# Constant products ahead of TensorE's waits in a Fourier-attention layer

## The chip, the cores and the metric

The kernel runs on one core of one Trainium2 chip. The metric is device time in microseconds (us) of one execution. A core has a matrix engine (TensorE, "PE" in the profile, with its weight loads as "PEld"), three elementwise engines (VectorE "DVE", ScalarE "ACT", GpSimd "POOL"), a queue engine (SyncE "SP") and 16 DMA engines. TensorE reads SBUF and writes PSUM. TensorE's clock is granted by a throttle: the profile shows the share granted, 1.00 or less.

## The reference

The input is `x` of shape (4, 32, 128, 128). Layer 0 is a Fourier neural operator with attention over the 32 images (128 x 128) of each of the four batch elements; layer 1 is an additive attention and a mixture of experts over 4096 tokens per batch element. Only layer 0 matters here:

```python
xn = _inorm(xa, norm1_w, norm1_b)
k = _fno_layer(xn, Kcw, Ksw, Hs, Ws); q = _fno_layer(xn, Qcw, Qsw, Hs, Ws)
v = _fno_layer(xn, Vcw, Vsw, H, W)
scores = jnp.einsum('bntk,bnsk->bnts', qf, kf) / (np.float32(np.sqrt(Hs * Ws)) * temperature)
p_attn = jax.nn.softmax(scores, axis=-1)
av = jnp.einsum('bnts,bnsk->bntk', p_attn, vf)
p = _fno_layer(av, Pcw, Psw, H, W)
a = _inorm(p + xa, attn_w, attn_b)
an = _inorm(a, norm2_w, norm2_b)
m = _fno_layer(an, m0cw, m0sw, H, W, inner_norm=True, act=True)
m = _fno_layer(m, m1cw, m1sw, H, W, inner_norm=True, act=False)
out = _inorm(m, mon_w, mon_b) + a
```

Each `_fno_layer` is a 2-D Fourier transform cut to a block of modes, a product with complex weights, and the transform back, plus a scaled copy of its input. The kernel does the transforms as products with matrices of cosines and sines, and works out the scores and the means and variances from the modes. All of it is float32.

## The kernel before, in words

`layer0` runs a loop over the four batch elements `b` (the loop begins at L687). For one `b` it goes through these stages, all on the 32 images of that element:

- attention-weighted values (`po`, L778): five blocks of modes, in each of which VectorE and GpSimd multiply modes with weights (`u`) and TensorE sums over the images with the probabilities `pr`; `cm` (L703) and the skips (`pxt` L723, `sk` L742) go with it;
- back to space (`py` L798, then `inverse`, L273 and L278), and the statistics of the sum `q`;
- the first inner layer: `spectra` (`pz` L248, `px` L871), then `weighed` (L894), in which VectorE reduces the weighed squares to `v_s` and TensorE sums over the partitions (`ms`, in `sums`, L314); then `back` (L288): products `y` (L297) into two wide PSUM tiles, a copy `v` to SBUF by ScalarE or VectorE, the product `four` (L308), and `gelu` by VectorE and ScalarE;
- the same for the second inner layer, with the next element's statistics (`image_sums`, whose matrix sums are `mg`, `bg` and `my`) and modes (`spectra_of_images`: `pz`, `px` L263 and L264) and its attention (`attention_weights`) between its parts; then `back` again with `last`, which adds to the output image.

`attention_weights` makes the scores. For each of 17 mode columns VectorE makes a tile `pa`, and VectorE (every third column) or GpSimd (the others) a tile `pb` (L522, L524), of 32 x 32 products of modes; TensorE sums both over the modes into `sp` (L528), four products of 32 rows each. `pa` and `pb` share six SBUF buffers, one of which holds `sod` through the stage. Then come `sc`, the softmax, and a way through DRAM (`prd`) that gives `pr`.

The statements are Python, but their order on the engines is not the text's: a scheduler places the instructions of layer 0 on each engine's queue, from its own estimates of when each is ready. Each queue then runs strictly in that order. A PSUM tile that is asked for under a tag (`a`, `b` and `wide`, two buffers each) waits until an older tile of that tag has been read. The orders on the queues that are told below are those of the built programs. Layer 1 has an order written out by hand, and is not touched.

In the first pass, before the loop, the weights for the values are prepared on VectorE (L469 to L479) beside the first element's statistics and modes, and the first attention.

Of the kernel before, what the change touches and what calls it, by code (L numbers as in the profile page):

```python
# [7 lines left out]
F32 = mybir.dt.float32  # L8
# [5 lines left out]
P = 128  # L14
# [94 lines left out]
def layer0(  # L109
    tc, x, kq_modes, kq_mirror, vcw, pcw, mcols, mcol0, mrows, heads, heads_row, small_row, by_p, inv_cols, dram, x1, first  # L110
):
    nc = tc.nc
# [174 lines left out]

    def back(spec, a, take):  # L288


        wide = [ps.tile([P, 2, 512], F32, name="y1", tag="wide") for _ in range(2)]
        for slot in range(4):
            c = slice(slot * P, slot * P + P)
            for k, trig in enumerate((cos_back, sin_back)):
                for g in range(4):
                    r = slice(32 * g, 32 * g + 32)
                    nc.tensor.matmul(  # L297
                        wide[g // 2][:, g % 2, c],
                        spec[r, 4 * a + slot, 64 - 64 * k : 192 - 64 * k],
                        trig[r],  # L300
                        start=k == 0,
                        stop=k == 1,
                    )
        for g in range(4):
            v = grp.tile([P, 4, C], F32, name="v1", tag="v", bufs=3)
            evacuate(v.rearrange("p k c -> p (k c)"), wide[g // 2][:, g % 2])
            four = ps.tile([P, 4, C], F32, name="four", tag="b")
            nc.tensor.matmul(four, inv, v, start=True, stop=True)  # L308
            take([image(a, g, k) for k in range(4)], four)

    def sums(name, matrix, src):

        m = ps.tile(list(src.shape), F32, name=name, tag="wide")
        nc.tensor.matmul(m, matrix, src, start=True, stop=True)  # L314
        return m

# [3 lines left out]
    def image_sums(b, xt):  # L320


        rows8 = ps.tile([64, 4, C], F32, name="rows8", tag="wide")
        for g in GROUPS:
            xx2 = grp.tile([P, GI, C], F32, name="xx2", tag="pr", bufs=6)
            nc.scalar.activation(xx2, xt[:, g : g + GI], AF.Square)
            for h in range(2):
                m = g // 4 + h
                for k, src in enumerate((xt[:, 4 * m : 4 * m + 4], xx2[:, 4 * h : 4 * h + 4])):
                    nc.tensor.matmul(  # L330
                        rows8[32 * k : 32 * k + 32],
                        one_of_8[:, 7 - m : 39 - m],
                        src,
                        start=m == 0,
                        stop=m == 7,
                    )
        ev = grp.tile([64, 4, C], F32, name="ev", tag="v", bufs=3)
        nc.scalar.copy(ev, rows8)
        s12 = ps.tile([P, 2, 512], F32, name="s12", tag="wide")[:, :, :T]
        for j in range(4):  # L340
            for k in range(2):
                r = slice(32 * k, 32 * k + 8)
                nc.tensor.matmul(s12[:, k, j::4], ev[r, j], ident[r, r], start=True, stop=True)
        sv = small.tile([P, 2, T], F32, name="sv", tag="pk_sq")
        nc.vector.tensor_copy(sv, s12)

        tot = one("tot", 2)
        nc.vector.tensor_reduce(tot, sv, AX.X, ALU.add)
        mg = sums("mg", group, tot)
        gm = one("gm")  # L350
        nc.vector.tensor_copy(gm, mg[:, 0:1])
        gv = one("gv")
        nc.vector.tensor_mul(gv, gm, gm)
        nc.vector.tensor_tensor(gv, mg[:, 1:2], gv, ALU.subtract)
        gr, _ = inv_std("gn_r", gv, 1)
        gs = one("gs")
        nc.vector.tensor_mul(gs, gm, gr)

        both = small.tile([P, 2, 32], F32, name="both", tag="both")
        nc.vector.tensor_scalar(both[:, 0], of_group, gr, None, ALU.mult)  # L360
        nc.vector.tensor_scalar(both[:, 1], of_group, gs, -1.0, ALU.mult, ALU.mult)
        by_group = small.tile([P, 2, 32], F32, name="by_group", tag="by_group")
        nc.vector.tensor_copy(by_group, sums("bg", ones, both))
        n = 1 + 2 * KY
        colg = small.tile([P, 2, n], F32, name="colg", tag="colg")
        nc.vector.tensor_scalar(colg[:, 0], cols1[:, :n], gr, None, ALU.mult)
        nc.vector.tensor_scalar(colg[:, 1], cols2[:, :n], gr, None, ALU.mult)
        m128 = one("m128")
        nc.vector.tensor_scalar(m128, gm, 128.0, None, ALU.mult)

        gs128 = one("gs128")
        nc.vector.tensor_scalar(gs128, gs, 128.0, None, ALU.mult)
        gg = one("gg")
        nc.vector.tensor_mul(gg, gs, gs128)
        gr2 = one("gr2")
        nc.vector.tensor_mul(gr2, gr, gr)
        grs = one("grs")
        nc.vector.tensor_scalar(grs, gs, gr, -2.0, ALU.mult, ALU.mult)
        y12 = small.tile([P, 2, T], F32, name="y12", tag="pk")
        nc.vector.tensor_scalar(y12[:, 0], sv[:, 0], gr, gs128, ALU.mult, ALU.subtract)  # L380
        nc.vector.tensor_scalar(y12[:, 1], sv[:, 1], gr2, gg, ALU.mult, ALU.add)
        nc.vector.scalar_tensor_tensor(
            y12[:, 1], sv[:, 0], grs, y12[:, 1], ALU.mult, ALU.add
        )
        nc.vector.tensor_scalar(y12, y12, 1.0 / NPIX, None, ALU.mult)
        my = sums("my", ones, y12)
        ym, yv = per_image("ym"), per_image("yv")
        nc.vector.tensor_copy(ym, my[:, 0])
        nc.vector.tensor_mul(yv, ym, ym)
        nc.vector.tensor_tensor(yv, my[:, 1], yv, ALU.subtract)  # L390
        yr, _ = inv_std("n1_r", yv)
        ysc = scalars(ALU.mult, "n1_s", yr, par[:, N1W : N1W + 1])
        return by_group, colg, m128, ysc
# [93 lines left out]
    def attention_weights(b, front):  # L487
# [23 lines left out]
        )  # L511

        sp = ps.tile([P, T, 16], F32, name="sp", tag="b")
        for yy in range(KA):
            xs_p = xp[:, yy].unsqueeze(2).to_broadcast(tt)
            xs_s = xm[:, yy].unsqueeze(2).to_broadcast(tt)
            pa = grp.tile(tt, F32, name="pa", tag="pr", bufs=6)
            pb = grp.tile(tt, F32, name="pb", tag="pr", bufs=6)
            for k, t in enumerate((pa, pb)):
                other = xm[:, k * KA + yy].unsqueeze(1).to_broadcast(tt)  # L520
                if k == 0 or yy % 3 == 2:
                    nc.vector.tensor_tensor(t, xs_p, other, ALU.mult)  # L522
                else:
                    nc.gpsimd.tensor_tensor(t, xs_s, other, ALU.mult)  # L524
            for j, (wt, pp, h) in enumerate(
                (w, p, h) for w, p in ((w_re, pa), (w_im, pb)) for h in range(2)
            ):
                nc.tensor.matmul(  # L528
                    sp[32 * j : 32 * j + 32],
                    wt[:, yy],  # L530
                    pp[:, :, 16 * h : 16 * h + 16],
                    start=yy == 0,
                    stop=yy == KA - 1,
                )
# [152 lines left out]
    for b in range(B):  # L687
# [12 lines left out]
        for h in range(2):  # L700
            r = slice(32 * h, 32 * h + 32)
            cm = ps.tile([P, T, 16], F32, name="cm", tag="a")
            nc.tensor.matmul(cm, pv[r].to_broadcast([NH, P]), ph[r], start=True, stop=True)  # L703
            cd = grp.tile([P, T, 16], F32, name="cd", tag="v", bufs=3)
            nc.vector.tensor_tensor(cd, cm, sel.unsqueeze(2).to_broadcast([P, T, 16]), ALU.mult)
            nc.vector.tensor_reduce(
                cp[:, 16 * h : 16 * h + 16], cd.rearrange("p s t -> p t s"), AX.X, ALU.add
            )
# [42 lines left out]
        for x0 in range(0, KX, NK):  # L751
            nk = min(NK, KX - x0)
            m = nk * KY
            po = ps.tile([P, NK * KY], F32, name="po", tag="a")[:, :m]
            for i in range(4):
                xb = late.tile([P, 2, NK * KY], F32, name="xb", tag="xb")[:, :, :m]
                for r in range(2):
# [133 lines left out]
                nc.scalar.activation(spec[:, s4, :64], spec[:, s4, P:], AF.Copy, scale=-1.0)  # L891
            return spec, sq

        def weighed(name, sq, squares, weights):  # L894

            t = sq[:, 1]
            by_row, by_column = weights
# [15 lines left out]
                ALU.mult,  # L913
            )
            nc.vector.scalar_tensor_tensor(by_t, squares, by_column, by_t, ALU.mult, ALU.add)
            m = sums("ms", ones, by_t)
            out = per_image(name)
            nc.vector.tensor_copy(out, m)
            return out


        spec, sq = spectra(0, q)
        v0 = weighed("v0", sq, squares, layers[0][2])
        nc.vector.tensor_mul(v0, v0, r2)
        nc.vector.tensor_mul(v0, v0, r2)
        r0, ve = inv_std("r0", v0)
# [40 lines left out]
        spec, sq = spectra(1, gl)  # L967
        if b + 1 < B:
            front = spectra_of_images(b + 1, loaded, normed)
        v1 = weighed("v1", sq, squares, layers[1][2])  # L970
        vc = weighed("vc", sq, squares, layers[1][3])
        r1, _ = inv_std("r1", v1)
        s1 = par[:, S1 : S1 + 1]
        nc.vector.tensor_mul(vc, vc, r1)
# [671 lines left out]
```

## Time and profile before

| | |
|---|---|
| median of 3 runs | 3178.72 us (3177.18 to 3182.71) |
| profiled execution, its own time | 3191.62 us |
| span of the profiled execution | 3189.9 us |
| mean granted TensorE clock, whole span | 0.953 |
| layer 0, 0 to 1105 us: TensorE busy, clock | 934.2 us, 0.87 |
| layer 1, 1105 to 3189.9 us: TensorE busy, clock | 1994.5 us, 0.99 |

The profile is of one execution. Its parts are the busy time of each engine by slice of the span, the waits of an engine with what ended them, the timeline of an engine's instructions (start, duration, engine, line, operation, out<-in, shapes, count, and in brackets the idle time before it and what ended that), and the busy time by stretch. In the waits the columns are the total, the number and the longest. A float32 product has two records in the trace, so a count of x16 is eight products. Ends of products are modelled; starts are not.

### The profile page before, as it was taken

To read this page: it belongs to the slowest core of one execution; us is meant where nothing else is said; L and a number is where in the kernel's file an instruction comes from. 1 tells how busy PE (TensorE), PEld (TensorE's weight loads), DVE (VectorE), ACT (ScalarE), POOL (GpSimd) and SP (SyncE) were. 2 spreads that over 40 slices of the span, in tenths; PEclk is the share of its full clock that TensorE was granted. 3 is DMA by queue.
4 is the path that set the end of the run, shared out by engine and by line. 5 is a ranking of instruction groups with operands and counts; after the bars stand their busy time and mean duration, and the time that the engine had idled before them with its cause. 6 is when DMAs were issued, how large, how long until landed. Compare 5 with 4: busy or idle time off the path is not lost.

```text
span 3189.9 us, 53099 instructions
## 1 busy us (share of the span) xinstructions
PE 2928.7 (92%) x19634; PEld 1438.2 (45%) x19634; DVE 2290.9 (72%) x5035; ACT 2311.7 (72%) x3138; POOL 2102.7 (66%) x1831
## 2 busy tenths in 40 slices
PE   7888798798888789999999999999999999999997
PEld 5366365345546444444344443444444444444443
DVE  5876666667677566777666868866778777687887
ACT  2344243253343589998999999998999999999992
POOL 1621540460451289878788797889878889888773
PEclk6998998899898799999999999999999999999998
DMA  6301310130140211010111010011010011101000
GB/s 140 111 18 30 95 50 3 49 123 1 30 130 2 57 31 31 8 31 7 31 37 24 14 24 14 8 39 31 23 29 9 14 37 24 37 1 31 14 14 14
DMA packets 152308, 112.77 MB, mean 35 GB/s; under 512 B 36878, under 2 KB 140657, under 8 KB 151441
## 3 DMA queue, kind: packets, MB, share of 16 engines
q1 hardware_dynamic: 136209, 103.61, 12.2%
q10 hardware_dynamic: 15840, 5.77, 0.8%
q8 instruction: 155, 2.54, 0.3%
q14 instruction: 104, 0.85, 0.1%
HBM read 68.37 MB, written 20.00 MB: 28 GB/s over the span
## 4 chain that ended last, share of the span: by engine, by line
PE 61%; POOL 12%; ACT 9%; DVE 9%; issue 7%; DMA 1%; ACTq 0%; POOLq 0%; DVEq 0%; SPq 0%
PE d L1446 19%; PE po L1465 11%; PE px L1352 6%; ACT r L1496 4%; PE po L778 4%; PE n L1446 3%; POOL e L1505 3%; POOL e L1504 3%; PE pz L248 2%; PE four L308 2%; ACT e L1512 2%; PE px L871 1%; PE sk L742 1%; POOL kx L1111 1%; DVE r L1501 1%
## 5 line engine op out<-in xcount | busy, mean ns | idle before, releaser
L1501 DVE TENSOR_TENSOR r<-n,r 128x1024 f32<-128x1024 f32 (+1 forms) x1056 | 961.6, 952 | 479.0 <-PE n L1446 389.4
L1504 POOL TENSOR_TENSOR e<-r 128x512 f32<-128x512 f32 x528 | 673.2, 1275 | 268.1 <-DVE r L1501 267.6
L1496 ACT ACTIVATE r<-d 128x1024 f32<-128x1024 f32 (+1 forms) x1056 | 792.9, 802 | 67.4 <-PE n L1446 56.4
L1508 ACT ACTIVATE r<-r 128x1536 f32<-128x1536 f32 x528 | 783.6, 1484 | 16.8
L1505 POOL TENSOR_TENSOR e<-e,r 128x512 f32<-128x512 f32 x528 | 671.3, 1271 | 41.4
L1446 PE MATMUL d<-qe,ke 32*128 32x512 f32 (+3 forms) x2304 | 605.8, 602 | 39.6 <-ACT r L1496 36.5
L1465 PE MATMUL po<-e,kx 128*128 128x512 f32 (+3 forms) x1152 | 594.5, 605 | 15.6 <-POOL e L1517 15.6
L1446 PE MATMUL n<-qe,ke 32*128 32x512 f32 (+3 forms) x2304 | 606.2, 601 | 0.0
L1446 PE MATMUL n<-qf,kf 32*128 32x512 f32 (+3 forms) x2304 | 552.6, 554 | 0.0
L1446 PE MATMUL d<-qf,kf 32*128 32x512 f32 (+3 forms) x2304 | 550.2, 553 | 0.0
L1356 DVE SCALAR_TENSOR_TENSOR xc<-px,wgt,xc 128x128 f32<-128x128 f32 x1024 | 358.1, 350 | 42.2 <-PE px L1352 9.7
L1512 ACT ACTIVATE e<-e 128x512 f32<-128x512 f32 x528 | 325.8, 617 | 66.2 <-POOL e L1505 65.6
L1465 PEld LDWEIGHTS po<-e,kx 128*128 128x128 f32 x1152 | 175.5, 188 | 392.8 <-issue 306.9
L1446 PEld LDWEIGHTS d<-qe,ke 32*128 32x128 f32 x2304 | 176.5, 183 | 359.3 <-ACT r L1496 339.5
L773 POOL TENSOR_TENSOR u<-xb,gb 128x858 f32<-128x858 f32 (+1 forms) x120 | 233.1, 1968 | 139.5 <-PE po L778 128.0
L1446 PEld LDWEIGHTS d<-qf,kf 32*128 32x128 f32 x2304 | 220.2, 186 | 176.1 <-issue 163.8
L1352 PE MATMUL px<-we,x2t 128*128 128x512 f32 x512 | 264.0, 601 | 6.8 <-DVE xc L1356 6.0
L775 DVE TENSOR_TENSOR u<-xw,gb 128x858 f32<-128x858 f32 (+1 forms) x200 | 206.6, 1082 | 59.2 <-PE po L778 46.6
L885 POOL TENSOR_TENSOR spec<-part,part 128x512 f32<-128x512 f32 x16 | 24.8, 1550 | 333.4 <-ACT z L188 75.2
L1446 PEld LDWEIGHTS n<-qf,kf 32*128 32x128 f32 x2304 | 228.3, 185 | 19.2 <-issue 11.4
L778 PE MATMUL po<-u,pr 128*32 128x429 f32 (+1 forms) x1280 | 191.1, 548 | 26.8 <-DVE u L775 11.7
L524 POOL TENSOR_TENSOR pb<-xm 128x1024 f32<-128x1024 f32 x48 | 90.7, 1913 | 159.1 <-ACT xm L457 152.8
(388 smaller groups left out, 3953.9 us busy)
## 6 DMA issues: line engine op xcount, KB each, us to landing
xb<-xd SPq DMA_DIRECT2D x128, 214.5 KB
xc<-x SPq DMA_DIRECT2D x29, 512.0 KB
x<-x SPq DMA_DIRECT2D x16, 512.0 KB
qf<-qe SPq DMA_DIRECT2D x64, 128.0 KB
out<-xc SPq DMA_DIRECT2D x15, 512.0 KB
xb<-xd SPq DMA_DIRECT2D x32, 198.0 KB
gb<-gd SPq DMA_DIRECT2D x4, 1056.0 KB
x<-in_x SPq DMA_DIRECT2D x8, 512.0 KB
```

What stands on the lines that cost most here:

```text
L773: nc.gpsimd.tensor_tensor(u, xb, gk, ALU.mult)
L778: nc.tensor.matmul(po[32 * j : 32 * j + 32], pr[:, i, k], u[:, r], start=i == 0 and k == 0, stop=i == 3 and k == 1,)
L1352: nc.tensor.matmul(px, x2t[:, k * P : (k + 1) * P], we[:, e0 : e0 + 4], start=True, stop=True)
L1356: nc.vector.scalar_tensor_tensor(xc[:, k], px[:, e], wgt[:, k, e0 + e : e0 + e + 1], xc[:, k], ALU.mult, ALU.add)
L1446: nc.tensor.matmul(o, k, q, start=turn == 0 or g > 0, stop=turn == 1 or g > 0)
L1465: nc.tensor.matmul(sums[c, h][:, q0 : q0 + c1 - c0], kx[:, jb], e[:, c0:c1], start=jb == 0, stop=is_last and q0 > 2 * P, skip_group_check= ...
L1496: nc.scalar.activation(r[:, g], d, AF.Ln, scale=1.0 / DSCALE)
L1501: nc.vector.tensor_tensor(r[:, g], part, r[:, g], ALU.mult)
L1504: nc.gpsimd.tensor_tensor(e, r[:, 1], r[:, 2], ALU.add)
L1505: nc.gpsimd.tensor_tensor(e, e, r[:, 0], ALU.add)
L1508: nc.scalar.activation(r, r, AF.Exp, scale=-1.0)
L1512: nc.scalar.activation(e, e, AF.Exp)
```

## The change

A function `hold(tile, n)` issues `n` products of two constant matrices (`rows` and `inv`, 128x128) into a PSUM tile that a later product overwrites. It is called in six places: ahead of the first `four` of each `back` (3), ahead of `bg` for the first element (18, into a tile of their own), for each of the 17 columns of `attention_weights` (4, into a tile `beside` of tag `b` that nobody reads), ahead of the two `cm` of the first element (26 and 8), ahead of the first block of `po` (14), and ahead of `ms` in the first inner layer and, for the last element, the second (24, the tile then being 128 columns wide instead of 32). In all 548 products are added:

| tile | products |
|---|---|
| `beside` | 272 |
| `ms` | 120 |
| `po` | 56 |
| `four` | 48 |
| `cm` | 34 |
| `early` | 18 |

No other instruction is added or removed; the scheduler's order changes in places on every engine.

```diff
             four = ps.tile([P, 4, C], F32, name="four", tag="b")
+            if g == 0:
+                hold(four[:, 0], 3)
             nc.tensor.matmul(four, inv, v, start=True, stop=True)
...
-    def sums(name, matrix, src):
+    def hold(tile, n):
+
+        for _ in range(n):
+            nc.tensor.matmul(tile, rows, inv[:, : tile.shape[-1]], start=True, stop=True)
+
+    def sums(name, matrix, src, idle=0):
 
-        m = ps.tile(list(src.shape), F32, name=name, tag="wide")
+        m = ps.tile([P, P] if idle else list(src.shape), F32, name=name, tag="wide")
+        if idle:
+            hold(m, idle)
+            m = m[:, : src.shape[-1]]
         nc.tensor.matmul(m, matrix, src, start=True, stop=True)
         return m
...
+        if b == 0:
+            hold(ps.tile([P, P], F32, name="early", tag="wide"), 18)
         nc.vector.tensor_copy(by_group, sums("bg", ones, both))
...
         sp = ps.tile([P, T, 16], F32, name="sp", tag="b")
+        beside = ps.tile([P, P], F32, name="beside", tag="b")
         for yy in range(KA):
+            hold(beside, 4)
...
             cm = ps.tile([P, T, 16], F32, name="cm", tag="a")
+            if b == 0:
+                hold(cm.rearrange("p s t -> p (s t)")[:, :P], 26 - 18 * h)
...
             po = ps.tile([P, NK * KY], F32, name="po", tag="a")[:, :m]
+            if x0 == 0:
+                hold(po[:, :P], 14)
...
-        def weighed(name, sq, squares, weights):
+        def weighed(name, sq, squares, weights, idle):
...
-            m = sums("ms", ones, by_t)
+            m = sums("ms", ones, by_t, idle)
...
-        v0 = weighed("v0", sq, squares, layers[0][2])
+        v0 = weighed("v0", sq, squares, layers[0][2], 24)
...
-        v1 = weighed("v1", sq, squares, layers[1][2])
-        vc = weighed("vc", sq, squares, layers[1][3])
+        v1 = weighed("v1", sq, squares, layers[1][2], 24 * (b + 1 == B))
+        vc = weighed("vc", sq, squares, layers[1][3], 0)
```

## The prediction

> **What bounds the kernel now.** I read the page's slices of the span first, then the waits of TensorE inside the first 1110 us, then TensorE's timeline and the busy time by stretch. The change touches layer 0 alone, which ends near 1105 us.
>
> ```profile
> PE   7888798798888789999999999999999999999997
> PEclk6998998899898799999999999999999999999998
> ```
> From about slice 15 on TensorE is full and its clock granted; before that the clock is short in most slices. The waits of TensorE in that part:
>
> ```profile
> PE ms L314 <- DVE v_s L915: 31.3, 5, 6.3
> PE sp L528 <- POOL pb L524: 23.6, 16, 2.4
> PE po L778 <- DVE u L775: 11.7, 4, 5.2
> ...
> PE cm L703 <- DVE ph L564: 9.5, 4, 7.7
> ...
> PE bg L314 <- DVE both L361: 4.5, 1, 4.5
> ```
> These are the "known waits": five of about 6 us for `ms`, four of 3 to 5 us for `po`, one of 7.7 for `cm`, one of 4.5 for `bg`, sixteen short ones for `pb`. What follows them is in the busy time by stretch (PE, PEld, DVE, ACT, POOL, then clock, DMA share, GB/s):
>
> ```profile
> 32.00:66.00 34.00, 32.41 (x148) 31.64 (x148) 15.72 (x59) 3.43 (x8) 0.00 (x0) 0.50 0.52 114
> 66.00:97.00 31.00, 28.11 (x172) 7.28 (x171) 29.25 (x37) 3.97 (x6) 23.37 (x13) 0.81 0.47 107
> 229.00:256.00 27.00, 24.73 (x179) 11.37 (x180) 22.10 (x95) 16.93 (x39) 0.00 (x0) 0.83 0.00 1
> 306.00:344.00 38.00, 28.32 (x178) 7.81 (x178) 28.41 (x32) 15.70 (x37) 33.53 (x17) 0.77 0.08 21
> 486.00:521.00 35.00, 32.43 (x176) 18.40 (x178) 23.21 (x98) 18.34 (x40) 0.00 (x0) 0.64 0.00 0
> ```
> At half clock TensorE looks busy because its products take twice as long. Only in 32:66 is TensorE itself the bound. In 229:256 and 486:521 (the gelu stage of the first two images) VectorE and ScalarE work beside it; in 66:97 (attention of the first batch element) VectorE is full, and in 306:344 (that of the second) GpSimd is.
>
> Durations come from TensorE's timeline:
>
> ```profile
> 190.64 1.96 PE L273 MATMUL pv<-cst,yf 128*66 128x128 f32 x16 [1.00 <-ACT yf L188]
> 192.44 2.02 PE L278 MATMUL four<-icol,v 66*128 66x128 f32 x16
> ...
> 260.90 0.62 PE L871 MATMUL px<-z,cst 128*32 128x256 f32 x2
> 261.45 0.49 PE L248 MATMUL pz<-cst,g 128*128 128x128 f32 x2
> 261.87 1.06 PE L871 MATMUL px<-z,cst 128*32 128x256 f32 x20
> ...
> 328.05 0.62 PE L528 MATMUL sp<-pb,w_im 128*32 128x512 f32 x2 [0.80 <-POOL pb L524]
> 328.06 0.62 PE L528 MATMUL sp<-pa,w_re 128*32 128x512 f32 x2
> 328.50 0.60 PE L528 MATMUL sp<-pb,w_im 128*32 128x512 f32 x2
> 328.52 0.60 PE L528 MATMUL sp<-pa,w_re 128*32 128x512 f32 x2
> 328.93 0.60 PE L528 MATMUL sp<-pb,w_im 128*32 128x512 f32 x2
> ```
> A product has two records. Eight 128x128 products in a row take 192.44 - 190.64 = 1.80 us, 0.225 each; a lone `pz` between two narrow `px` takes 261.87 - 261.45 = 0.42, so 0.2 more. The lone `px` of 256 columns takes 0.55; `sp` runs its four 32-row products of 512 columns side by side in 0.88 (328.05 to 328.93), so 256 columns should be 0.43: another 0.12. A lone full-width product inside narrow ones thus costs 0.225 + 0.32.
>
> **The Trainium skill.** "TensorE: Matmul & The Clock Gate", Part 1, "What's actually happening": the clock is halved by default and is released by about 3.4 us of activity, lost after an idle window. The trace agrees on 1.00 and 0.50, but in 32:66 the clock stays at 0.50 though products of 67 columns follow one another: not every busy stretch releases it. The same page, "LDWEIGHTS (loading the stationary operand)": the load's time is set by the columns of the weights; the trace agrees, since `px` of 67 columns is 0.22 at full clock, like the 0.225 above. Part 3, "The mechanism": products start and end in program order; so an added product that runs late delays the one that it stands ahead of. The trace shows no product out of the program's order. "Why this matters for your kernels" asks for no idle gap over about 3 us; here a gap of 2.2 us (317.9 to 320.1) already cost the clock.
>
> **The change, part by part.** 548 full-width products are added: 126 us of TensorE at 0.23, twice that at half clock.
>
> *Waits for `ms`* (24 each, 5 waits). 24 x 0.23 = 5.5 us inside 6.0 to 6.3: free, and the clock should be whole when `y` and `four` follow. Worth: VectorE's waits for `four` while the clock is low. In 229:256 these are 0.16 + 0.88 + 0.21 = 1.2 us; in 486:521 they sum to 11.3 against 4.4 in 229:256, so 7 there; about 2 in each of the later two. VectorE's `v` and `x` instructions stand in fixed order before the first `g` (it would start at 235.6 instead of 235.7), so the rest of the 4 us that TensorE saves is idle time. TensorE then idles 2 us before the third `four`, and may lose the clock again, as at 494 us: I take 8 of the 12. The fifth wait (1064 to 1070) is followed by gaps of 2.5 and 4.1 us for `v`, which throw the clock away again: -2 (0 to -8, from 12 us of lost cycles in 1070:1105).
>
> *`po`* (14, 4 times): 3.2 us in waits of 3 to 5.2; lost cycles after them are 1.3, 2.9 and 1.7 us, half on the path: -3. *`four`* (3, 16 times): 0.42 + 2 x 0.225 = 0.87 against a wait of 0.3 to 0.6 after the copy of `v`; where VectorE is the bound nothing is lost, in the second use of `back` about 0.3 each: +2.
>
> *`beside`* (4 for each of 17 columns, 4 times). In the changed order on TensorE, 9 stand before `so`, 12 between `so` and the first `sp`, and 47 among the `sp` in 20 groups; in four columns a group also stands between `pa` and `pb`, which then no longer run side by side. `beside` takes the PSUM buffer of the last `px`, so it starts when VectorE has copied that, at 306.5, when `so` starts now; and the clock is at half there. 9 x 0.45 = 4.05, `so` 1.5, 12 holds 2.9 (clock back by then): first `sp` near 315 instead of 311.9. From there 13 x 0.86 + 4 x 1.72 = 18.1 for `sp`, 47 x 0.225 = 10.6, 20 x 0.32 = 6.4: 35.1 us, ends at 350.1; now 343.4. GpSimd's own work (12 `pb` of 1.9, 4 adds of 2.35: 32.3 from 309.0) no longer covers it: TensorE becomes the bound. Softmax, `y`, `four` and `po` queue behind `sp` on TensorE, VectorE's `mx` behind `pa`: all move by 7. Three times: +21. What is unmeasured is the cost of a lone hold among `sp`: without any switching cost 28.7 us, end 344 to 346 with GpSimd's waits: +1 to +2.5 each; with the groups at half clock much more.
>
> *First batch element.* The 18 `early` fill 19.2 to 23.3; `bg` comes at 23.4 instead of 30.6, since VectorE's chain to `both` is now ahead of the value weights. But `my` now stands before `px`, and waits for `y` behind six 32x1088 instructions of 0.7 to 1.27 us: near 33. TensorE is idle from 24.6, the clock is lost as before, `px` starts 2 us later, and 8 `pz` (0.45 each) come later: `so` 4.4 us later if the clock stays low; 7 us earlier if the run of 11 `pz` (5 us) brings it back. Then `sp`: 35.1 us in place of 25 (72.2 to 97.0). Less 2.3 us (constants on VectorE kept `mx` from 101.1 to 103.5, now done meanwhile) and 2 us of full clock for `cm` and `po` (27 holds, 6.2 us in a wait of 7.7): +13 in the one case, -1 in the other; I take +6.5.
>
> Sum: 6.5 + 21 + 2 - 8 - 3 - 2 = +16.5 us. Queues of DMA issues change little: the loads of layer 1's `spare` move two places ahead of `xb`, `prd` behind two more copies of `xw` on ScalarE (1 us, inside the above).
>
> **Time.** The profiled execution took 3191.6 us (span 3189.9), the median of the three runs is 3178.7. 3191.6 + 16.5 = 3208; on the median 3195.
>
> **Rivals.** (1) *Faster: a lone hold costs only its 0.225 and the clock stays whole.* Then `sp` is covered by GpSimd again: 3 x 2.5 + 1, gelu stage -12, `po` -4, the last element -8, `four` 0: about -16, median 3163. It decides where the switch costs under about 0.1 us. For it: the sums above lean on five lone `pz`; against: each of those shows 0.42. 0.25.
> (2) *No change to speak of:* the first element gains its clock (-1), switching costs half (3 x 4), gains as taken: -1 + 12 + 2 - 13 = 0, 3179. 0.15.
> (3) *The change does not do what it says:* the holds do not keep the clock, gelu gains nothing: 13 + 27 + 2 = +42, 3221; if they stay at half clock inside `sp`, an attention stage takes 13 x 1.7 + 4 x 3.4 + 47 x 0.45 + 6 = 63 us, over +100 in all. The lone half-clock stretch 32:66 speaks for it, against it that the 3.3 us of `pz` from 822 us brought the clock back. 0.15. The forecast itself: 0.45.
>
> By itself the forecast's case runs from 3185 (first element -1, TensorE's stream two us shorter) to 3206 (first element +13). The range 3160 to 3226 leaves out the tails of (1) and (3). A difference of 0.2% (6.4 us) is about what a measurement of this kernel can tell from none. Faster 0.25, same 0.15, slower 0.60.
>
> **What would show it.** Right: no idle of TensorE before `ms`, clock 1.00 in the gelu stages; `sp` in each attention stage 35 us long with waits of VectorE and GpSimd for `sp` grown from some 6 and 0.7 us; a lone hold of 0.4 us. Wrong: `sp` still ending with GpSimd's last `pb`, or the clock back in 32:66.

## The result and the profile after

| | before | after |
|---|---|---|
| median | 3179.22 us (3177.18 to 3182.71) | 3205.37 us (3204.40 to 3207.38) |
| ratio, 95% interval | | 1.0082 (1.0064 to 1.0099) |
| profiled execution, its own time | 3191.62 us | 3205.44 us |
| end of layer 0 in it | 1104.4 us | 1116.9 us |
| rest of the span | 2085.5 us | 2086.8 us |

The changed kernel is 26 us slower. Of the 13.8 us between the two profiled executions 12.5 lie in layer 0; layer 1 is nearly as long in both. The profiled execution of before lies 12 us above its median, that of after on its median, so the two traces show only half of the difference; how far executions of one kernel differ is taken up below, at the kernel before once more. One execution of the kernel before among those of the experiments, 3229.20 us at a clock of 0.913 where its others have 0.950 to 0.965, is in a slower state and is left out of every comparison.

The slices of the span of after: first TensorE's busy share, then its granted clock.

```profile
PE   7999999999999889999999999998999999999997
PEclk9999999999999899999999999999999999999998
```

In the first 15 slices the clock's digits 6 and 8 of before have become 9, and its 7 an 8: the products do what they are there for, TensorE is fuller and its clock is granted. The kernel is slower all the same. The waits of TensorE in 0 to 1140 us (total, number, longest):

```profile
PE four L309 <- DVE v L190: 13.3, 8, 2.7
...
PE my L323 <- DVE y L396: 7.7, 1, 7.7
...
PE po L795 <- DVE u L792: 4.1, 5, 1.1
...
PE ms L323 <- DVE v_s L932: 3.6, 5, 1.3
...
PE cm L718 <- DVE ph L577: 1.8, 1, 1.8
PE po L315 <- DVE cd L720: 1.8, 1, 1.8
```

The known waits have shrunk (`ms` from 31.3 to 3.6, `cm` from 9.5 to 1.8, `po` for `u` from 11.7 to 4.1) or are gone (`bg`, 4.5 before), `my` has the new wait that the prediction named, and `sp <- POOL pb`, 23.6 before, isn't there any more. Turned round, who waited for `sp` (same columns), before:

```profile
DVE pa L522 <- PE sp L528: 18.3, 17, 2.7
POOL pb L524 <- PE sp L528: 4.8, 7, 2.6
```

and after:

```profile
POOL pb L537 <- PE sp L541: 34.5, 13, 3.4
DVE pb L535 <- PE sp L541: 18.0, 16, 1.3
DVE pa L535 <- PE sp L541: 12.2, 16, 1.4
```

In the attention stage TensorE used to wait for GpSimd; now GpSimd and VectorE wait for TensorE. The busy time by stretch of after (PE, PEld, DVE, ACT, POOL, then clock, DMA share, GB/s):

```profile
34.00:66.00 32.00, 29.60 (x229) 28.93 (x230) 18.99 (x69) 8.99 (x15) 1.46 (x1) 0.82 0.54 112
239.00:269.00 30.00, 25.34 (x205) 12.19 (x204) 24.78 (x104) 19.79 (x43) 0.00 (x0) 1.00 0.01 1
319.00:360.00 41.00, 41.00 (x290) 20.15 (x288) 26.84 (x23) 13.30 (x35) 33.79 (x17) 1.00 0.04 12
501.00:536.00 35.00, 31.97 (x234) 16.99 (x232) 25.89 (x104) 20.37 (x44) 0.00 (x0) 0.95 0.00 1
```

In the attention stage (third line) TensorE has 41.00 us of work in 41, at full clock. In the gelu stages (second and fourth) the clock is 1.00 and 0.95 where it was 0.83 and 0.64. In the first batch element (first line) it is back for more than half of the stretch; there it was 0.50 throughout.

Where layer 0's time lies, from the starts in TensorE's timelines, each row but the first and last summed over the batch elements (us):

| stretch | before | after | no `beside` | only `beside` | only `ms` |
|---|---|---|---|---|---|
| start to first `so` | 66.8 | 63.5 | 64.5 | 71.9 | 67.0 |
| `so` to end of `sp` | 141.6 | 163.2 | 142.6 | 164.3 | 139.9 |
| end of `sp` to `po` | 99.8 | 112.0 | 110.8 | 101.5 | 101.7 |
| `po` to `py` | 274.4 | 266.8 | 268.1 | 270.8 | 273.1 |
| `py` to the next `so` | 384.9 | 380.9 | 372.2 | 380.7 | 375.6 |
| last `py` to the end | 136.9 | 130.5 | 130.7 | 134.2 | 127.0 |
| sum | 1104.4 | 1116.9 | 1088.8 | 1123.5 | 1084.4 |

Each column is one execution; the label of a run stands below with its edit. The medians in the text are those of many executions.

### The profile page after: what moved, and what is told of

The parts are those of the page before. It is cut to its first block, busy times and chain, and to the rows that moved or that the text cites. A ratio compares the mean times of both kernels' runs of the same rounds, so it can differ in the third digit from the quotient of the medians.

```text
span 3203.7 us, 55305 instructions
## 1 busy us (share of the span) xinstructions
PE 3018.5 (94%) x20730; PEld 1536.9 (48%) x20730; DVE 2295.3 (72%) x5035; ACT 2312.2 (72%) x3138; POOL 2102.9 (66%) x1831
## 4 chain that ended last, share of the span: by engine, by line
PE 66%; POOL 10%; ACT 9%; DVE 9%; issue 5%; DMA 1%; ACTq 0%; POOLq 0%; DVEq 0%; SPq 0%
PE d L1463 19%; PE po L1482 11%; PE px L1369 6%; ACT r L1513 4%; PE po L795 4%; PE n L1463 4%; POOL e L1522 3%; PE pz L248 3%; POOL e L1521 3%; PE sp L541 3%; PE beside L315 2%; PE four L309 2%; PE px L888 2%; ACT e L1529 2%; POOL kx L1128 1%
## 5 line engine op out<-in xcount | busy, mean ns | idle before, releaser
L1463 PEld LDWEIGHTS n<-qf,kf 32*128 32x128 f32 x2304 | 228.2, 185 | 20.0 <-issue 12.5
L795 PE MATMUL po<-u,pr 128*32 128x429 f32 (+1 forms) x1280 | 182.1, 525 | 14.2 <-POOL u L790 9.1
```

Source lines behind the costliest of these rows:

```text
L795: nc.tensor.matmul(po[32 * j : 32 * j + 32], pr[:, i, k], u[:, r], start=i == 0 and k == 0, stop=i == 3 and k == 1,)
L1463: nc.tensor.matmul(o, k, q, start=turn == 0 or g > 0, stop=turn == 1 or g > 0)
```

## The experiments

**Theory.** The loss is the 68 products of `beside` in each attention stage, and in them the passage between products with 128 columns of weights and those with 32, which makes TensorE the bound of that stage. **Rivals:** the loss lies in the first element's new order and in products that run at half clock; it goes by the number of products; or it comes from the PSUM buffer that `beside` takes.

### Without `beside`, and `beside` alone

```diff
# no_beside, against the changed kernel
-        beside = ps.tile([P, P], F32, name="beside", tag="b")
-            hold(beside, 4)
# only_beside: the kernel before with these two lines and hold()
```

> The changed kernel without the tile `beside` and its 68 products per attention stage; all other products stay. Theory (the lone full-width products among the 32-column ones make TensorE the bound of the attention stage): `sp` is about 31.5 us long again in the second to fourth batch element instead of 35 to 37, ends with GpSimd's last `pb`, and the products ahead of `so` are gone (3 us each): 3205 - 25 = 3180 us, 3174 to 3185. Rival (the products' worth is the clock, and the loss lies elsewhere, in the first element and in `po` products that run at half clock): the attention stage stays at half clock, `po` products cost more, and the time stays at 3195 or above.

> The kernel before with the tile `beside` and its 68 products per attention stage, nothing else. Theory: `sp` 35 us long in the four attention stages instead of 25 and three times 31.6, and about 3 us ahead of each `so`; some 2 us come back before `py` each time: 3179 + 26 = 3205 us, 3197 to 3212. Rival (the loss lies in the first element's order and in the other products): at most 3190 us.

Measured: without `beside` 3170.54 us, 0.9981 (0.9972 to 0.9991) of before; `beside` alone 3213.60 us, 1.0103 (1.0082 to 1.0124). Taken away it is worth 1.0082 / 0.9981 = 1.0101, or 32 us; added alone it costs 33 us. So `beside` is more than the whole loss, and all the other products together gain 6 us. Both lie just outside the ranges that the theory gave (3174 to 3185 and 3197 to 3212), and on the side that makes `beside` dearer still; the values of the rival, 3195 or more and 3190 or less, are far off. The waits of the kernel without `beside`:

```profile
PE sp L539 <- POOL pb L535: 19.9, 18, 2.3
```

GpSimd is the bound of `sp` again. In the table, `beside` puts 20.6 us between `so` and the end of `sp` (163.2 against 142.6) and 8.7 ahead of `so` (380.9 against 372.2), where 9 or 10 products stand behind the last `px`.

Taking `beside` away is not quite clean, because the scheduler then moves other constant products to where it stood: in the built program 15 of the 34 `cm` products now stand among the `sp` of the first element, in 8 groups, and that `sp` stage takes 28.0 us, where the kernel before needs 25.2 and the changed kernel 35.3. The next experiment, `narrow`, leaves the order alone.

### The same places, 32 columns wide; and fewer of them

```diff
# narrow
-            hold(beside, 4)
+            for _ in range(4):
+                nc.tensor.matmul(beside[:32], rows[:, :32], inv[:, :P], start=True, stop=True)
# beside1
-            hold(beside, 4)
+            hold(beside, 1)
```

> The changed kernel with the 68 products of `beside` made 32 columns wide in their weights (`rows[:, :32]` into the first 32 partitions of the tile), in the same places and the same number: 9 ahead of `so`, 12 ahead of the first `sp`, 47 in the same 20 groups among the `sp`. Theory (what costs is the passage between products of 128 and of 32 columns of weights, 0.32 us a group): no passages are left among the `sp`, each stage of `sp` is back near 31.5 us with GpSimd as its bound, 4 us less four times, while the 9 products ahead of `so` still cost 3 us each: 3189 us, 3183 to 3195. Rival (the number of products and their order behind VectorE's and GpSimd's tiles cost, whatever their width): `sp` still 35 us, 3202 us or more.

> The changed kernel with 1 product of `beside` for each of the 17 columns instead of 4. In TensorE's order 9 (or 10) of them stand ahead of `so` and the rest between `so` and the first `sp`, none among the `sp`. Theory: the `sp` stage is 31.5 us long again, what is left of the cost is 3 us ahead of each `so`: 3171 (the kernel without `beside`) + 12 = 3183 us, 3178 to 3190. Rival (the cost goes by the number of products): 3171 + 35/4 = 3179, 3175 to 3182, with `so` not later than without them. Third (the lost time is not TensorE's order but the PSUM buffer that the tile takes): 3200 or more.

Measured: `narrow` 3177.02 us, 0.9991 (0.9980 to 1.0001) of before; `beside1` 3184.01 us, 1.0007 (0.9998 to 1.0016). In the built programs `narrow` has the order of the changed kernel to the instruction, on every engine, and of the 32 us only some 3 are left (its interval and that of the kernel without `beside` overlap). Number, order and PSUM buffer are the same, so none of these three is the loss. One passage in the timeline of the changed kernel:

```profile
325.49 0.62 PE L541 MATMUL sp<-pa,w_re 128*32 128x512 f32 x2
325.51 0.62 PE L541 MATMUL sp<-pb,w_im 128*32 128x512 f32 x2
325.95 0.60 PE L541 MATMUL sp<-pa,w_re 128*32 128x512 f32 x2
325.96 0.60 PE L541 MATMUL sp<-pb,w_im 128*32 128x512 f32 x2
326.49 0.49 PE L315 MATMUL beside<-cst 128*128 128x128 f32 x2
326.91 1.05 PE L541 MATMUL sp<-pa,w_re 128*32 128x512 f32 x4
```

and in `narrow`:

```profile
309.48 0.62 PE L542 MATMUL sp<-pa,w_re 128*32 128x512 f32 x2
309.50 0.62 PE L542 MATMUL sp<-pb,w_im 128*32 128x512 f32 x2
309.91 0.62 PE L542 MATMUL sp<-pa,w_re 128*32 128x512 f32 x2
309.95 0.60 PE L542 MATMUL sp<-pb,w_im 128*32 128x512 f32 x2
310.34 0.38 PE L528 MATMUL beside<-cst 128*32 128x128 f32 x2
...
310.54 0.62 PE L542 MATMUL sp<-pb,w_im 128*32 128x512 f32 x2
```

Two halves of a column that follow one another stand 0.44 apart. With a full-width product between, from 325.95 to 326.91, they stand 0.96 apart: 0.52 for one product that takes 0.225 in a row. With a narrow one, from 309.91 to 310.54, it is 0.63: 0.19 to 0.20. A longer group pays the 0.3 us once: with groups of 1, 2, 5 and 6 full-width products it is 0.96, 1.18, 1.84 and 2.06 us from `sp` to `sp` in the changed kernel (medians of 42, 16, 16 and 4 places at full clock), which is 0.44, 0.223 for each product, and 0.29 to 0.30. The Trainium skill, "TensorEngine Tiling (Array Packing)", "Key Properties", says that changing the tiling mode drains TensorE; these two places agree with it, and put 0.3 us on going there and back. What happens inside TensorE in that time no run here shows. What follows from it by stretch (`narrow`, columns as above):

```profile
305.00:340.00 35.00, 32.12 (x290) 18.64 (x288) 26.72 (x23) 12.51 (x32) 32.87 (x17) 0.98 0.05 14
```

As many products as in 319:360 of the changed kernel (x290), but in 35 us, with GpSimd at 32.87 as the bound and the clock at 0.98. Summed over the elements, `so` to the end of `sp` takes 140.2 us, no more than the 142.6 without any. The four `sp` stages are not alike, though: they take 25.3, 29.4, 34.7 and 32.1 us. In the third TensorE waits 2.91 us for a `pb` of GpSimd at 583.75 us, and the clock is at half from 582.6 to 589.4: the narrow products in these places did not keep it there. I had expected 3189, from 4 us less four times; the first element alone got 10 back (its `sp` takes 25.3 us again), and all four 23 (163.2 to 140.2). The products ahead of `so` are still there, 2.2 to 4.1 us for 9 or 10; `py` to the next `so` takes 376.9 us against 372.2, in one trace of each.

`beside1` has no product of `beside` among the `sp`. Its `sp` stages of the second to fourth element take 30.4, 29.8 and 31.8 us, as before. In the first element it takes 33.0, and the reason is a second test of the theory, which the edit brought with it: the scheduler has put 32 of the `cm` products among those `sp`, in 16 groups.

```profile
68.29 0.62 PE L541 MATMUL sp<-pa,w_re 128*32 128x512 f32 x2
...
68.75 0.60 PE L541 MATMUL sp<-pa,w_re 128*32 128x512 f32 x2
...
69.29 0.49 PE L315 MATMUL cm<-cst 128*128 128x128 f32 x2
69.71 0.62 PE L541 MATMUL sp<-pa,w_re 128*32 128x512 f32 x2
```

From 68.75 to 69.71 it is 0.96 us again, 0.52 for the one product, and this tile lies in a PSUM buffer of another tag. The first `sp` stage takes 25.2 us with no full-width products among the `sp`, 28.0 with 15 in 8 groups, 33.0 with 32 in 16 and 35.3 with 47 in 20.

`beside1` costs about 8 us more than no `beside` (1.0007 against 0.9981). The theory gave 12 for the products ahead of `so`, a cost by number 9, and 4.8 of the 8 come from the `cm` products in the first element (`so` to the end of `sp` 38.1 us against 33.3), which neither had in it. So by its time it separates nothing; the length of `sp` speaks for the theory. The third expectation, the PSUM buffer, would have shown in both kernels, and did not.

### The products ahead of `ms` alone

```diff
-            m = sums("ms", ones, by_t)
+            m = sums("ms", ones, by_t, idle)
# 24 for v0, 24 * (b + 1 == B) for v1, 0 for vc; nothing else of the change
```

> The kernel before with the 24 products ahead of `ms` alone (five waits). Theory: TensorE has no idle time before `ms`, its clock is 1.00 in the gelu stage, and 4 to 12 us of VectorE's waits for `four` go: 3171 us, 3167 to 3175. Rival (the time that TensorE saves turns into idle time behind VectorE's and ScalarE's own work): within 0.2%, 3174 to 3183 us.

Measured: 3173.36 us, 0.9980 (0.9968 to 0.9993): 6 us faster, near the 3171. The waits of this kernel:

```profile
PE four L307 <- DVE v L190: 15.8, 9, 3.3
PE four L307 <- ACT v L188: 9.4, 9, 4.1
...
PE ms L321 <- DVE v_s L922: 3.6, 5, 1.3
```

The waits for `ms` are down from 31.3 us to 3.6, but `four` still waits, up to 4.1 us, for the copies of VectorE and ScalarE, which take as long as before (0.68 and 0.59 us each). The prediction looked for the gain in VectorE's waits for `four` and `y` in the gelu stages. In the 35 us from `ms` on these are, over the four elements, 23.8, 17.4 and 11.1 us in the traces without the `ms` products (before twice, `early` alone, below) and 17.7, 13.8, 16.3 and 19.8 in those with them and without `beside` (`ms` alone, `ms` with `early`, no `beside`, no `beside` and no `po`): no gain that shows. After the fifth wait, in the last element's second `back`, the same waits are 9.1, 8.9 and 8.9 us without and 4.7, 3.6, 4.3 and 4.3 with them. That is 5 us, and nearly all of the 6 us of the medians.

### The kernel before once more

> The kernel before, unchanged, profiled once more. If the 12 us by which its profiled execution lay above the median were chance, the span is now near 3178 us and the clock of the whole span above 0.953; if profiling itself slows this kernel, it is near 3190 again. Time: 3179 us, within 0.2%.

Measured: 3179.17 us, 1.0005 (0.9994 to 1.0017); span of the profiled execution 3186.4 us, clock 0.952. So the span did not fall near 3178. Profiling as such is no cause that shows: of the other profiled executions some lie above the median of their kernel (`ms_gap` 3178.40, `no_po` 3216.14), some below (`only_early` 3172.61, `narrow` 3173.04). Executions of the kernel before ran from 3169.10 us (clock 0.964) to 3193.74 (0.950), and the two profiled ones lie in the upper half of that. The two traces show that stretches move both ways: `py` to the next `so` of the second element took 132.2 us in the first and 126.0 in the second, but the end of `sp` to `po`, over the four elements, 99.8 and 106.9. The first of these holds the 7 us that the prediction read from 486:521: VectorE's waits for `four` and `y` after that `ms` are 11.3 us in the first trace, 6.4 in the second, and 1.7 in the one with `early` alone.

What makes executions differ is open. In all 13 traces the clock has only the two values 1.00 and 0.50, and it changes only at whole multiples of 3.41 us from one another; a gap that falls a little otherwise between these steps may cost the clock in one execution and not in the next, but no run here tests that.

### The products of the first element

```diff
# only_early: the kernel before with
+        if b == 0:
+            hold(ps.tile([P, P], F32, name="early", tag="wide"), 18)
# ms_early: this and the products ahead of ms
```

> The kernel before with the 18 products of `early` ahead of the first `bg` alone. TensorE's order is then that of the changed kernel up to the second half of `px`: `my` ahead of `px`, 11 `pz` in one run between the two halves. Theory: that run brings the clock back near 45 us, `so` of the first batch element comes at about 64 instead of 67, and the end moves by as much: 3176 us, 3172 to 3179. Rival (the later start of `px` wins): `so` at 67 or later, 3179 to 3185.

> The kernel before with the 24 products ahead of `ms` and the 18 of `early`, no others. If the two gains are independent: 3173 - 3 = 3170 us, 3166 to 3174; if the first element's shift is absorbed later: that of `ms` alone, 3173.

Measured: `early` alone 3181.40 us, 0.9999 (0.9984 to 1.0013); with `ms` 3175.24 us, 0.9981 (0.9968 to 0.9995), no better than `ms` alone. The run of 11 `pz` at 41 to 45.6 us does bring the clock back, and `so` comes at 61.8 instead of 66.8 us. Of these 5 us most are lost again ahead of the softmax. ScalarE's timeline with `early` alone:

```profile
94.30 0.52 ACT L776 COPY xw<-xb 128x429 f32<-128x429 f32 x1 [29.43 <-DMA xb<-xd]
95.23 0.52 ACT L776 COPY xw<-xb 128x429 f32<-128x429 f32 x1 [0.41 <-DMA xb<-xd]
95.69 0.58 ACT L545 COPY spt<-sp 128x512 f32<-128x512 f32 x1
```

`sp` ends at 92.3, but its copy `spt` stands behind two copies of `xw`, which wait for a load that lands at 94.3. TensorE's next product says what that costs:

```profile
96.32 1.87 PE L556 MATMUL sc<-spt,cst 128*32 128x512 f32 x2 [3.98 <-ACT spt L545]
```

In the kernel before, `spt` waits 0.46 us for `sp` itself. The gap takes the clock away too (1.87 us for this product, 1.05 before), and `po` starts 1.6 us earlier instead of 5. In this kernel an earlier `so` is worth next to nothing as long as these loads come when they do. In the changed kernel the loads hold nothing up, because its `sp` ends later:

```profile
103.85 0.59 ACT L549 COPY spt<-sp 128x512 f32<-128x512 f32 x1 [3.39 <-PE sp L541]
```

### The products ahead of `po`

```diff
-            if x0 == 0:
-                hold(po[:, :P], 14)
# no_beside_po: from the kernel without beside; no_po: from the changed kernel
```

> The kernel without `beside` and without the 14 products ahead of `po` as well (left: `early`, `cm`, `four`, `ms`). In the run without `beside` those 14 took 5.4, 5.0, 3.9 and 3.3 us, the first two at half clock, and `po` began 1 us or more after its `u`. Theory A (they cost as much as the full clock after them gives back): 3171 us in the scale of a kernel before of 3179, 0.998 of it, within 0.15%. Theory B (the -3 us of the prediction is there): 3174 us or more. Theory C (products that themselves run at half clock delay `po` for nothing): 3166 us or less.

> The changed kernel without the 14 products ahead of `po` alone. In the changed kernel they took 6.2 us at half clock in the first batch element, where `po` began 13.7 us later than before, and 3.3 to 4.8 us in the others. Theory: `po` of the first element begins 5 us earlier, the others gain 0 to 1 us and lose as much after them: 3205 - 4 = 3201 us. Rival (they restore the clock for `po`, as predicted): 3208 us.

Measured: without `beside` and `po` 3171.98 us, 0.9979 (0.9970 to 0.9988), as with the `po` products (0.9981); from the changed kernel 3205.10 us, 1.0076 (1.0061 to 1.0090) against 1.0082. They are worth nothing either way, and the 4 us that I expected of the second were not there. The first of the two kernels has `early`, `cm`, `four` and `ms` left, and is no different from `ms` with `early` (0.9981), so `cm` and `four` together are worth nothing that shows either. The timeline of the changed kernel shows both sides:

```profile
121.35 6.17 PE L315 MATMUL po<-cst 128*128 128x128 f32 x28
...
383.71 3.29 PE L315 MATMUL po<-cst 128*128 128x128 f32 x28
...
653.28 4.81 PE L315 MATMUL po<-cst 128*128 128x128 f32 x28 [1.82 <-DVE cd L720]
```

In the first element they run at half clock, 0.42 to 0.44 each, and `po` starts at 127.5; without them it starts at 121.35. From the end of `sp` to `po` they cost 7.1 us in the four elements (112.0 against 104.9), and from `po` to `py` they give 9.3 back (266.8 against 276.1). The trace without them is of an execution 11 us above its median, so these sums are rough; in the medians nothing of them is left.

### Products in the gaps after `ms` as well

```diff
# ms_gap: the kernel before with the products ahead of ms, and in back()
+            if g < 2:
+                hold(four[:, 0], idle[g])
# idle: (0, 9) for gelu's first half, (12, 16) for the last element's first half of `last`
```

> The kernel before with the 24 products ahead of `ms`, and products in the waits for `v` that follow it: 9 ahead of the second `four` of the gelu stage (a wait of 2.5 to 3.3 us), 12 and 16 ahead of the first two `four` of the last element (waits of 3.2 and 4.1 us). Theory (the clock that the gap takes away is worth what the prediction took for it, the 4 of 12 us it left out): no stretch at half clock between the second `four` and the end of the gelu stage, 3173 - 4 = 3169 us, 0.997 of the kernel before. Rival (VectorE and ScalarE bound these stages, so the clock is worth nothing more there): 0.998, as with the products ahead of `ms` alone.

Measured: 3165.55 us, 0.9961 (0.9945 to 0.9978), the lowest median of all (of 7 executions): faster than before by 7 to 17 us, where 0.997 was expected. Against `ms` alone (0.9980) the intervals overlap, so that this step adds something is likely and not shown. Its timeline:

```profile
232.56 1.12 PE L309 MATMUL four<-v,cst 128*128 128x512 f32 x2 [0.51 <-ACT v L188]
233.52 2.17 PE L315 MATMUL four<-cst 128*128 128x128 f32 x18
236.13 2.22 PE L309 MATMUL four<-v,cst 128*128 128x512 f32 x4 [0.44 <-DVE v L190]
```

The gap of 2.45 us that stands ahead of the second `four` in the kernel with `ms` alone is filled, and the wait left is 0.44. These products have the width of `four` on both sides. The stretch is still not whole, though: a later `four` of the same stage runs at 1.5 us a product, after 1.7 us without work. And in the last element the edit doesn't do what it was meant to: the scheduler puts 11 of these products ahead of `y`, TensorE still waits 3.36 us for `v` ahead of the first `four`, VectorE's waits are 9.4 us, as without any products, and last `py` to the end takes 137.7 us. This trace is of the slowest of the 7 executions (3178.40 us), so it can't say where the lower median comes from.

## Why the prediction was right and wrong

The forecast was slower, 3195 us; measured 3205. Its sum was +16.5 us; the medians differ by 26, the two profiled executions by 13.8. By parts, sorted by what the experiments could separate (us):

| part | predicted | measured |
|---|---|---|
| `beside`: 3 x 7, and the 10 that `sp` grows in the first element | +31 | +32 (taken away), +33 (alone) |
| `ms`: -8 and -2 | -10 | -6 (-10 to -2) |
| first element otherwise: 6.5 - 10 | -3.5 | 0 (-5 to +4) |
| `po` | -3 | 0 |
| `four` | +2 | not run alone; 0 together with `cm` |

**`beside`: right, in size and mechanism.** A lone product costs 0.225 + 0.30 (predicted 0.225 + 0.32); `sp` takes 35.3, 35.3, 36.8 and 35.9 us (predicted 35.1); TensorE is the bound in GpSimd's place; and in the second to fourth element the first `sp` comes 8.3, 9.1 and 8.9 us after the end of the last `px`, where it was 5.9: near the +3. One step did not happen: `beside` does not wait for VectorE's copy of the last `px`, it follows that `px` at once (315.62). And the eight products in a row that gave the 0.225 have 66 columns of weights, not 128; the constant products, which have 128, take 0.223 in a row, so nothing came of it. What was left out is that the 12 products between `so` and `sp` cost nothing, because they take the room of the 1.30 us wait for `sod` and of the first `sc`, which moves behind `sp`. The 9 ahead of `so` carry it.

**The gains: right in direction, too large, and in part by luck.** The term of the sum that failed is the -8 for the `ms` stages. It leaned on 7 us of waits in the second element of one execution, of which a second trace of the same kernel has 2 (6.4 us there, 4.2 in the first element), and VectorE's waits in these stages are no shorter with the products than without. The 6 us come from the last element instead, where the prediction had put -2: VectorE's waits there fall by some 5, and in the changed kernel its second `back` is shorter by 5.1 (from `ms` to the end, 34.4 to 29.3). So the total of -10 is near the measured -6 for another reason than the one given.

**The first element: right sign of its warm case, wrong worth.** Both named steps happened: `my` waits 7.7 us for `y` till 35.0, and the run of `pz` brings the clock back; `so` came 3.3 us earlier (the warm case had 7). The prediction then carried the shift through to the end. With `early` alone it isn't carried, because ScalarE's queue holds `spt` behind a load that was not in the working. In the changed kernel that load is no hindrance; there it is the way from the end of `sp` to `po` that grows, from 16.4 us to 23.7, and 6.1 of these 7.3 us are the `po` products at half clock. The 2.3 us for `mx` came only in part: it starts 1.75 us after the last `sc`, 2.4 before. Two sums of the working don't come out as written: its cold case is 4.4 + 10 - 2.3 - 2 = 10, not 13, and 3195 with a first element of +13 in place of +6.5 is 3202, not 3206. The measured 3205 lies above the one and just inside the other.

**`po`: failed.** The -3 counted the lost cycles after the waits, and not that the products run at half clock themselves after a gap of 1.8 us, and delay `po`.

**The rivals.** (1) needed a switch under 0.1 us; it is 0.3. (3) needed a clock that stays low; it came back. (2) needed half the switching cost. The signs named for a right forecast appeared, with 3.6 us of idle time left ahead of `ms` and a clock of 0.95 in the second gelu stage; of the signs for a wrong one, `sp` ending with GpSimd did not appear, and the clock back in 32:66 did, but was worth nothing. Behind the gains that were put too high stands one error: lost clock was taken for lost time. TensorE's busy time with the missing share of its clock, added up over layer 0 in stretches of 5 us, is 109 us before, 80 with `ms` alone, 62 without `beside`, 37 after and 35 in `narrow`; the medians are 3179, 3173, 3171, 3205 and 3177.

## What to carry to other kernels

By these runs, a product that only keeps the clock should have the tile width of the products around it, and stand in a wait where TensorE itself is needed next: lone full-width ones among 32-column ones cost more than twice their own time and made an engine that had time to spare the bound, narrow ones in the same places cost almost nothing. When such products are put in or taken out, look at where the scheduler then places the others. Where another engine sets the pace (GpSimd in the attention stage) a full clock buys nothing, so read lost clock only where TensorE ends the chain. And a gain read from one profiled execution must be seen in a second one, when executions differ by more than the gain.

## What the runs showed of the hardware

- One full-width product among 32-column ones cost 0.52 us, a 32-column product in the same place 0.19 to 0.20. The prediction had the first by inference from five lone products; the second was new.
- The granted clock is 1.00 or 0.50, and changes only at whole multiples of 3.41 us from one another, in all 13 traces.
- A gap of 1.8 us can be enough to lose the clock, and need not be. In the kernel before, a gap of 1.93 us ahead of a `four` at 245.24 did not lose it (1.00 from 238.2 to 299.6). In the third element of the changed kernel, 14 constant products right after a gap of 1.82 took 4.81 us: the clock was at half from 652.9 to 656.3, one step of 3.4 us, so that the first 7 ran at half clock. That agrees with the 3.4 us of activity that the Trainium skill, "TensorE: Matmul & The Clock Gate", Part 1, "What's actually happening", gives. In the first element, where products of `cm` follow the gap first, all 14 ran at half clock, 6.17 us. There the clock was low for three steps, from 117.0 to 127.2, though TensorE was busy in each (columns as above):

```profile
117.02:120.43 3.41, 3.41 (x11) 2.28 (x10) 1.70 (x2) 0.00 (x0) 0.00 (x0) 0.50 0.44 41
120.43:123.84 3.41, 3.41 (x13) 2.49 (x12) 2.28 (x5) 0.00 (x0) 0.00 (x0) 0.50 0.25 40
123.84:127.26 3.42, 3.42 (x19) 3.42 (x17) 0.87 (x1) 0.00 (x0) 0.00 (x0) 0.51 0.00 0
127.26:130.67 3.41, 3.41 (x53) 2.25 (x51) 1.61 (x2) 0.76 (x2) 1.96 (x1) 1.00 0.02 5
```

Of the three steps at half clock only the third has constant products from end to end, and the clock came back after it. What counts as activity is open.
